# A factored interaction network on one core: the four 64-row matmuls of a pair, issued two and two instead of all together

## The chip, the core and the metric

The kernel runs on one core of a Trainium2 chip. The metric is the device time of one execution in microseconds (us). Three executions of the kernel before gave 449.19, 449.53 and 449.75 us, so the median is 449.53 us. The profile that the document reads is of one further execution, which took 450.12 us; the span that its trace covers is 448.3 us, and the 1.8 us between the two lie outside the records.

## What is computed

The reference is a "compressed interaction network" over x of shape (1024, 64, 16): three layers, each of which multiplies every field of x with every field of the layer's input and contracts the products with a weight matrix. Cut to what matters:

```python
x0 = h = x                                          # (B=1024, F=64, E=16)
for i in range(3):                                  # W0: 128 x 4096, W1 and W2: 128 x 4096
    z = einsum('bfe,bge->bfge', x0, h).reshape(B, F * fh, E)
    y = einsum('oc,bce->boe', W[i], z) + b[i]
    x_i, h = (y[:, :64], y[:, 64:]) if i < 2 else (y, y)
    xs.append(x_i)
out = concat(xs, 1).sum(axis=2) @ fc_w.T + fc_b     # (B, 1)
```

## The kernel before

All data is fp32. The batch is cut into 32 chunks of 32 rows; a chunk has 32 x 16 = 512 columns (batch and embedding together). The kernel doesn't form all products of fields: it lays x out so that a product of two 128-row tiles (`z` blocks of 128 x 4 x 512, made on VectorE and GpSimd) holds pairs of fields at a fixed distance, and TensorE contracts those blocks with rearranged weights (`w_all`, `ws`).

Six chunks are done by a head (chunks 0 to 5; the first of them also build the rearranged weights) and by a tail; the other 26 are done as 13 pairs, `k` = 3 to 15. A pair's two chunks share products and sums of products, so that some contractions serve both. Each contraction is a matmul of 128 rows (the partitions that are summed over) by 64 columns (outputs) over 512 moving columns. Two outputs of 64 columns lie in the two column halves of the array and of a PSUM bank: half 0 is output partitions 0 to 63, half 1 is 64 to 127. For a pair, `p["A"]` is the half of chunk `b`, `p["O"]` that of chunk `a`: `A` is half 0 for even `k` and half 1 for odd `k`. The sums lie in the PSUM banks `alpha` (L605), `delta` (L608), `gamma` (L611) and `beta` (L614), each in one half of its bank.

TensorE's order is written by hand. `at(when, fn, ...)` (L516) puts a job on a list with a time; at the end of `cin_kernel` the list is sorted by that time and each job is recorded in turn, so that `when` fixes the order of the instructions on every engine and nothing else. `zipped(when, columns...)` (L519) takes two lists of jobs and interleaves them: job `m` of the first list at `when + m`, job `m` of the second at `when + m + 0.5`. One such couple of jobs, one per column half, is called a slot here. `window` (L741) zips the two lists of one pair, `a_column` (everything that goes to half `A`) and `o_column` (everything that goes to half `O`), in such an order that the first list is always that of half 0. The 13 windows come from `first_window` (L748, `k` = 3), `o_leads` (L771, odd `k`) and `a_leads` (L759, even `k`), each with 29 slots, the first with 27.

Not every term has 128 rows. The squares of single fields (`es[c]`: x in partitions 0 to 63, x squared in 64 to 127) go through four matmuls of 64 rows by 64 columns for each pair, issued by `squares` (L734): `h_extra` (L565) multiplies the lower half of `es[c]` (rows 64 to 127) into `alpha` for chunk `b` and into `delta` for chunk `a`; `v0x` (L572) multiplies its upper half (rows 0 to 63) into a bank `y` of its own. Chunk `b`'s two write half `A`, chunk `a`'s two write half `O`. So the four cover the four quarters of the array, and `squares` issues them one after the other at `t + 22.9`, between slot 22 and slot 23 of the window (in the last window at `t + 30.2`, after its last slot).

Other engines work around this: VectorE makes the products (L642) and adds the factors (L680 to L690), ScalarE copies operands into PSUM (L554) and takes snapshots of the sums (L669 to L675), GpSimd adds and subtracts product blocks (`w_mix`, L651, its operation at L659), and SyncE issues the loads. A `z` block is handed out by `take` (L87) from the front of a list of free blocks, and comes back to its end by `used` (L92) when the last matmul that reads it has been recorded; so the order in which matmuls are recorded also settles which block a later product gets.

All matmuls of the windows go through `mm` (L525), so their rows in the profile have the line L526, and are told apart by their tiles: `alpha<-e,vs` and `delta<-e,vs` are the two of `h_extra`, `y<-e,v` the two of `v0x`.

Of the kernel before, what the change touches and what calls it, by code (L numbers as in the profile page):

```python
# [70 lines left out]
def cin_kernel(ctx, tc, xra, xrb, wh, w0r, w1h, w2t, wx1, wx0, vec, out):  # L71
# [297 lines left out]
    for h in range(2):  # L369
        at = slice(32 * h, 32 * h + 32)  # L370
# [145 lines left out]
    def at(when, fn, *args, **flags):  # L516
        ops.append((when, len(ops), fn, args, flags))

    def zipped(when, *columns):  # L519
        for n, column in enumerate(columns):  # L520
            for m, job in enumerate(column):
                if job is not None:
                    at(when + m + n / len(columns), *job)

    def mm(out, w, rhs, start=False, stop=False):  # L525
        nc.tensor.matmul(out, w, rhs, start=start, stop=stop, skip_group_check=True)  # L526
# [38 lines left out]
    def h_extra(c, out=None, start=False):  # L565
        out = accs[c] if out is None else out
        mm(out[halves[c % 2]], w0ds[halves[1]], es[c][halves[1]], start=start)

    def new_y(k, tag):
        ys[k] = ps.tile([128, N], F32, tag=tag, name=f"y_{k}", bufs=4 if tag == "acc" else 2)  # L570

    def v0x(c, tag):  # L572
        if c // 2 not in ys:
            new_y(c // 2, tag)
        mm(ys[c // 2][halves[c % 2]], v0[halves[0]], es[c][halves[0]], start=True, stop=True)
# [49 lines left out]
    def w_run(p, out, w, name, start=False, at_t=0, order=GROUPS):  # L625
        return [
            (w_job, p, out, w, j * NI + i + at_t, name, start and n == 0)
            for n, (j, i) in enumerate(order)
        ]

    def p1_run(p, order, start=True):
        return w_run(p, alpha, wq_all, "X", start, order=order)

    def p7_run(p, order, start=True):
        return w_run(p, delta, s3, "T3", start, order=order)
# [85 lines left out]
    def p4_run(p):  # L721
        return w_run(p, delta, wh_all, "T2", at_t=2 * NI)

    def first_fill(p):
        return [(lambda: q_extra(p["a"], va, p["beta"]),)] + p4_run(p)[-LATE : -LATE // 2]

    def second_fill(p):
        return p4_run(p)[-LATE // 2 :]

    def late_run(p, out=alpha, first=0, last=2 * NI):  # L730
        jobs = w_run(p, out, s4, "B22", out is gamma)[first:last]
        return jobs if last < 2 * NI else jobs + [(lambda: q_extra(p["b"], vb, p["alpha"]),)]

    def squares(p):  # L734
        a, b = p["a"], p["b"]
        h_extra(b, p["alpha"])
        h_extra(a, p["delta"])
        v0x(b, "set")
        v0x(a, "set")

    def window(t, p, a_column, o_column, p1, p7, u2, quads=22.9):  # L741
        zipped(t, *(a_column, o_column)[:: -1 if p["k"] % 2 else 1])
        at(t + quads, squares, p)
        at(t + p1 - 0.4, snap_p1, p)
        at(t + p7 - 0.2, snap_p7, p)
        at(t + u2 - 0.4, snap_u2, p)

    def first_window(t, p, after, left):  # L748
        window(
            t, p,  # L750
            p1_run(p, GROUPS) + left[1][:1] + [(q_extra, 4, va)] + w_run(p, alpha, s2, "T2")
            + left[1][1:] + w_run(p, alpha, s1, "T3"),
            p7_run(p, GROUPS) + left[0][:1] + [(q_extra, 5, va)]
            + w_run(p, beta, wq_all, "B21", True, 2 * NI) + left[0][1:]
            + p1_run(after, FIRST_ROW) + p4_run(p)[:-LATE],
            8, 8, 18,
        )

    def a_leads(t, p, before, after):  # L759
        fill = first_fill(before)  # L760
        window(
            t, p,
            p1_run(p, SECOND_ROW, False) + fill[:1] + w_run(p, alpha, s2, "T2", order=FIRST_ROW)
            + fill[1:] + w_run(p, alpha, s2, "T2", order=SECOND_ROW) + second_fill(before)
            + w_run(p, alpha, s1, "T3") + p7_run(after, FIRST_ROW),
            p7_run(p, GROUPS) + late_run(before) + w_run(p, beta, wq_all, "B21", True, 2 * NI)
            + p4_run(p)[:-LATE],
            4, 8, 15,
        )

    def o_leads(t, p, before, after):  # L771
        last = after is None
        window(
            t, p,
            p1_run(p, SECOND_ROW + FIRST_ROW) + first_fill(before) + w_run(p, alpha, s2, "T2")
            + second_fill(before) + w_run(p, alpha, s1, "T3"),
            p7_run(p, SECOND_ROW, False) + late_run(before)
            + w_run(p, beta, wq_all, "B21", True, 2 * NI)
            + (late_run(p, gamma, 0, NI) if last else p1_run(after, FIRST_ROW))
            + p4_run(p)[:-LATE],  # L780
            8, 4, 19, 30.2 if last else 22.9,
        )

    def end_pair(t, p, whens):
# [93 lines left out]
    for n, p in enumerate(pairs):  # L878
        t = T0 + SPAN * n
        q, after = pairs[n - 1], pairs[n + 1] if n + 1 < NPAIR else None  # L880
        if n == 0:
            load_pair(t, p, -39.9, -33.3, -39.8, -27)
            make_pair(
                t, p, (-23.4, -20.7, -20.4, -16.5, -17.2, -16.8, -16.6, -7, -13.5, 3),
                (-14, -6.9, -6.8, 7.2, 12.4, 17.6, 17.5),
            )
            first_window(
                t, p, after, [[(contract_half, 5, 3, i, h) for i in (2, 3)] for h in range(2)]
            )
        else:  # L890
            load_pair(t, p, -34, -28, -27.8, -27.7)
            make_pair(
                t, p, (-21.4, -18.7, -18.4, -15.8, -12.2, -9.5, -6.1, -2, 1.6, 4.2),
                (-5, 1.6, 3.6, 7.2, 12.4, 18.6, 18.5),
            )
            (a_leads if n % 2 else o_leads)(t, p, q, after)
            end_pair(t, q, (0.7, 11.7, 17.9, 22.3, 23.2, 18.4, 36))
# [40 lines left out]
    t, q = T0 + SPAN * NPAIR, pairs[-1]  # L938
# [98 lines left out]
    last = cuts[1]  # L1037
# [84 lines left out]
```

## Time and profile before

| what | value |
|---|---|
| executions | 449.19, 449.53, 449.75 us |
| median | 449.53 us |
| profiled execution, its own time | 450.12 us |
| its span | 448.3 us |
| TensorE (PE) busy | 443.8 us, 99% of the span |
| VectorE (DVE) busy | 391.3 us, 87% |
| GpSimd (POOL) busy | 364.4 us, 81% |
| ScalarE (ACT) busy | 115.8 us, 26% |
| granted TensorE clock | 1.00 |

The page gives for each engine the busy time, its share of the span and the number of instructions. "PE" is TensorE's matmuls, "PEld" its weight loads, which have records of their own. One fp32 matmul of the program is executed as two passes over its moving columns, and each pass has one record as a matmul and one as a weight load. The ends of matmuls are modelled (a pass over 512 columns is recorded as 0.59 us long, and the next one on the same half starts 0.43 us after it), so TensorE's pace is read from starts, not from durations. A row of the timeline gives the start in us from the start of the span, the duration, engine, line, operation, the tiles (written<-read), rows*columns of the array where it is TensorE, the shape and type, and how many equal records in sequence were merged.

### The profile page before, as it was taken

The page shows a single profiled execution, that of the slowest core. Times are in us where ns is not written, and L with a number is a line of the kernel's source. Part 1 is how long each engine was busy: PE and PEld are TensorE (multiplying, and loading weights), DVE is VectorE, ACT ScalarE, POOL GpSimd, SP SyncE. Part 2 cuts the span into 40 slices and gives each one's busy share as a digit, 9 for nine tenths or more (in the row PEclk, how much of TensorE's full clock was granted, in tenths as well). Part 3 has the DMA queues.
Part 4 walks back from the last instruction along what each step waited for, and adds up shares of the span by engine and source line. Part 5 has one row for each costly group of instructions (what it writes and reads, how often), then busy time and mean ns, then how long its engine had stood idle before and what let it go on. Part 6 is the DMA issues. An engine that isn't in the chain of part 4 may idle for free.

```text
span 448.3 us, 6065 instructions
## 1 busy us (share of the span) xinstructions
PE 443.8 (99%) x2302; PEld 166.3 (37%) x2302; DVE 391.3 (87%) x284; ACT 115.8 (26%) x215; POOL 364.4 (81%) x125
## 2 busy tenths in 40 slices
PE   8999999999999999999999999999999999999997
PEld 4466343333333334333333333333333333333345
DVE  3996499989989989999899979999899998999644
ACT  2153151332222223131222222222231312222211
POOL 5413699998997979899797989979798997979920
PEclk9999999999999999999999999999999999999999
DMA  8987899298939587694958869495876939682500
GB/s 296 415 299 172 312 415 361 80 347 146 351 97 298 182 209 270 135 362 97 283 193 203 289 122 361 105 289 181 210 272 137 371 89 277 240 223 94 107 0 2
DMA packets 34484, 99.67 MB, mean 222 GB/s; under 512 B 6324, under 2 KB 6996, under 8 KB 27864
## 3 DMA queue, kind: packets, MB, share of 16 engines
q1 hardware_dynamic: 31800, 84.70, 53.4%
q0 software_dynamic: 1872, 13.63, 17.2%
q10 hardware_dynamic: 784, 0.95, 0.8%
q8 instruction: 18, 0.29, 0.3%
q14 instruction: 10, 0.08, 0.1%
HBM read 84.00 MB, written 1.64 MB: 191 GB/s over the span
## 4 chain that ended last, share of the span: by engine, by line
PE 98%; POOL 1%; ACT 0%; DVE 0%; issue 0%; POOLq 0%
PE alpha L526 45%; PE delta L526 20%; PE beta L526 11%; PE acc L526 7%; PE acc L252 6%; PE q L526 3%; PE acc L270 3%; POOL z L242 1%; PE misc L115 1%; PE xp L221 1%; PE y L526 0%; PE pv L359 0%; PE pm L386 0%; PE hx L526 0%; ACT xb_gps L314 0%; PE pc L924 0%
## 5 line engine op out<-in xcount | busy, mean ns | idle before, releaser
L659 POOL TENSOR_TENSOR z<-z,z 128x2048 f32<-128x2048 f32 (+1 forms) x78 | 299.6, 3872 | 30.5 <-PE alpha L526 30.5
L526 PE MATMUL alpha<-z,ws 128*64 128x512 f32 x624 | 240.8, 593 | 0.0
L642 DVE TENSOR_TENSOR z<-xa,xp 128x2048 f32<-128x2048 f32 x103 | 231.5, 2279 | 1.2
L526 PEld LDWEIGHTS alpha<-z,ws 128*64 128x64 f32 x624 | 75.2, 137 | 87.5 <-issue 84.8
L526 PE MATMUL delta<-z,w_all 128*64 128x512 f32 x208 | 95.5, 592 | 0.0
L526 PE MATMUL alpha<-z,w_all 128*64 128x512 f32 x208 | 93.5, 594 | 0.0
L526 PE MATMUL beta<-z,w_all 128*64 128x512 f32 x208 | 92.7, 594 | 0.0
L526 PE MATMUL delta<-z,ws 128*64 128x512 f32 x208 | 92.1, 594 | 0.0
L554 ACT COPY xp<-xb 128x512 f32<-128x512 f32 x88 | 51.4, 586 | 129.3 <-DVE z L642 110.8
L242 DVE TENSOR_TENSOR z<-xa,xp 128x2048 f32<-128x2048 f32 (+2 forms) x23 | 45.0, 2002 | 6.1 <-ACT xp L554 4.6
L242 POOL TENSOR_TENSOR z<-xa,xb 128x2048 f32<-128x2048 f32 x6 | 27.5, 4645 | 19.4 <-DMA xb<-in_xrb 19.4
L526 PEld LDWEIGHTS alpha<-z,w_all 128*64 128x64 f32 x208 | 28.0, 137 | 32.3 <-issue 29.2
L526 PEld LDWEIGHTS delta<-z,w_all 128*64 128x64 f32 x208 | 28.4, 137 | 30.8 <-issue 30.8
L526 PEld LDWEIGHTS beta<-z,w_all 128*64 128x64 f32 x208 | 28.0, 137 | 27.4 <-issue 27.4
L526 PEld LDWEIGHTS delta<-z,ws 128*64 128x64 f32 x208 | 27.9, 137 | 27.4 <-issue 25.7
L252 PE MATMUL acc<-z,w_all 128*64 128x256 f32 x256 | 29.0, 381 | 1.3 <-DVE z L242 1.2
L526 PE MATMUL acc<-z,w_all 128*64 128x512 f32 (+1 forms) x96 | 28.4, 594 | 0.0
L252 PEld LDWEIGHTS acc<-z,w_all 128*64 128x64 f32 x256 | 18.0, 137 | 13.6 <-DVE z L242 2.7
L673 ACT ACTIVATE snap<-alpha,vs 64x512 f32<-64x512 f32 x13 | 8.9, 682 | 50.1 <-PE alpha L526 50.1
L680 DVE SCALAR_TENSOR_TENSOR snap<-alpha,vs,snap 64x512 f32<-64x512 f32 x13 | 9.7, 747 | 12.4 <-PE alpha L526 12.3
L670 ACT COPY snap<-alpha 64x512 f32<-64x512 f32 x13 | 7.5, 580 | 48.7 <-PE delta L526 34.4
L294 DVE TENSOR_REDUCE acc<-uu 128x64 f32<-128x1024 f32 (+2 forms) x19 | 19.6, 1036 | 0.2
(117 smaller groups left out, 355.8 us busy)
## 6 DMA issues: line engine op xcount, KB each, us to landing
xa<-in_xra SPq DMA_DIRECT2D x32, 1024.0 KB, 8.9
xb<-in_xrb SPq DMA_DIRECT2D x128, 256.0 KB, 8.2
z<-z POOLq DMA_DIRECT2D x13, 1024.0 KB, 8.4
e<-in_xra SPq DMA_DIRECT2D x28, 128.0 KB, 8.1
xx<-in_xra SPq DMA_DIRECT2D x28, 128.0 KB, 3.1
z<-in_w2t SPq DMA_DIRECT2D x2, 1024.0 KB
z<-in_wx SPq DMA_DIRECT2D x2, 1024.0 KB, 9.1
z<-in_w1h SPq DMA_DIRECT2D x1, 1024.0 KB
```

The costliest lines, as they stand in the source:

```text
L115: nc.tensor.matmul(misc[:, 0:n], zeros, zeros[:, 0:n], start=True, stop=True)
L242: engine.tensor_tensor(blocks[zs[c, j]][:, at, :], xas[c][:, at, :], xbs[c][j].unsqueeze(1).to_broadcast([128, last - first, N]), ALU.mult,)
L252: nc.tensor.matmul(accs[c][halves[n]], w_all[:, t, 0:64], blocks[zs[c, j]][:, i, n * H2 : (n + 1) * H2], start=(t == 0), stop=(j == last a ...
L270: nc.tensor.matmul(accs[c][halves[1 - c % 2]], w_all[:, t, 64:128], blocks[zs[c, j]][:, i, :], start=(t == 0), stop=False, skip_group_chec ...
L294: nc.vector.tensor_reduce(acc[rows, of, k, half], uu[rows, of if at is None else at, E * half.start : E * half.stop].rearrange("p k (b e) ...
L526: nc.tensor.matmul(out, w, rhs, start=start, stop=stop, skip_group_check=True)
L554: nc.scalar.copy(bank, xbs[c][j])
L642: engine.tensor_tensor(blocks[b], xas[c], xbs[c][j].unsqueeze(1).to_broadcast([128, NI, N]), ALU.mult)
L659: nc.gpsimd.tensor_tensor(*(blocks[b][:, first:last] for b in (o, x, y)), ALU.subtract if in1 == "T3" else ALU.add,)
L670: nc.scalar.copy(snaps[0][p["O"]], alpha(p))
L673: nc.scalar.activation(snaps[1][p["O"]], alpha(p), AF.Identity, bias=bh1[p["A"]])
L680: nc.vector.scalar_tensor_tensor(hb_, alpha(p), bh1[p["A"]], hb_, ALU.add, ALU.add)
```

## The change

`squares` now issues the two matmuls of one chunk only: `h_extra` and `v0x` of that chunk, which write the same column half. `window` splits the zipped lists at `cut`, which is slot 23: slots 0 to 22 are zipped as before. Then come the two 64-row matmuls of half 0's chunk (`order[0]`), the half-1 job of slot 23, the half-0 job of slot 23, the two 64-row matmuls of half 1's chunk (`order[1]`), and then the remaining slots, each with its half-1 job first. In the last window the lists end before the cut, so that there the four 64-row matmuls stay together, in a new order (half 0's two, then half 1's two). No instruction is added or taken away on any engine.

```diff
-    def squares(p):
-        a, b = p["a"], p["b"]
-        h_extra(b, p["alpha"])
-        h_extra(a, p["delta"])
-        v0x(b, "set")
-        v0x(a, "set")
-
-    def window(t, p, a_column, o_column, p1, p7, u2, quads=22.9):
-        zipped(t, *(a_column, o_column)[:: -1 if p["k"] % 2 else 1])
-        at(t + quads, squares, p)
+    def squares(p, c):
+        h_extra(c, p["alpha" if c == p["b"] else "delta"])
+        v0x(c, "set")
+
+    def window(t, p, a_column, o_column, p1, p7, u2, quads=22):
+        columns, order = (a_column, o_column), (p["b"], p["a"])
+        if p["k"] % 2:
+            columns, order = columns[::-1], order[::-1]
+        cut = min(quads + 1, len(columns[0]))
+        zipped(t, columns[0][:cut], columns[1][:cut])
+        at(t + quads + 0.9, squares, p, order[0])
+        for m in range(cut, len(columns[0])):
+            at(t + m - 0.04, *columns[1][m])
+            at(t + m + 0.04, *columns[0][m])
+            if m == cut:
+                at(t + m + 0.08, squares, p, order[1])
+        if cut == len(columns[0]):
+            at(t + quads + 0.95, squares, p, order[1])
         at(t + p1 - 0.4, snap_p1, p)
         at(t + p7 - 0.2, snap_p7, p)
         at(t + u2 - 0.4, snap_u2, p)
...
-            8, 4, 19, 30.2 if last else 22.9,
+            8, 4, 19, 29.3 if last else 22,
```

## The prediction, as it was put on record before the changed kernel ran

> **What bounds the kernel now.** I read three views, from the widest to the closest: the page's busy times and its chain of work, the busy times stage by stage, and the timeline of TensorE around one issue of `squares`.
>
> ```profile
> PE 443.8 (99%) x2302; PEld 166.3 (37%) x2302; DVE 391.3 (87%) x284; ACT 115.8 (26%) x215; POOL 364.4 (81%) x125
> ...
> PE 98%; POOL 1%; ACT 0%; DVE 0%; issue 0%; POOLq 0%
> ```
>
> The first line alone proves little, since matmul records are modelled long. The second does more: followed back from the last instruction, 98% of the span was spent on TensorE with nothing else to wait for. So what TensorE spends or saves in its own stream goes to the end, as long as the others keep up.
>
> ```profile
> 131.00:157.06 26.06, 26.06 (x126) 8.46 (x124) 24.99 (x19) 6.33 (x11) 23.49 (x8) 1.00 0.74 222
> 157.06:183.24 26.18, 26.18 (x126) 9.38 (x125) 23.65 (x17) 6.21 (x11) 23.77 (x8) 1.00 0.73 221
> ```
>
> These are two stages, each from one issue of the four 64-row matmuls to the next, with the busy times of PE, PEld, DVE, ACT and POOL after the length; then the granted clock (1.00, so nothing here is throttled). Each is 29 slots and one `squares`, and the stages from 131.0 to 392.2 us repeat these two lengths. VectorE and GpSimd have at least 1 us of air in 26; GpSimd waits for TensorE 12 times, 30.5 us together. They follow, TensorE leads.
>
> ```profile
> 130.01 0.59 PE L526 MATMUL alpha<-z,ws 128*64 128x512 f32 x1
> 130.05 0.59 PE L526 MATMUL beta<-z,w_all 128*64 128x512 f32 x1
> 130.44 0.59 PE L526 MATMUL alpha<-z,ws 128*64 128x512 f32 x1
> 130.48 0.59 PE L526 MATMUL beta<-z,w_all 128*64 128x512 f32 x1
> 131.00 0.64 PE L526 MATMUL alpha<-e,vs 64*64 64x512 f32 x1
> 131.01 0.64 PE L526 MATMUL delta<-e,vs 64*64 64x512 f32 x1
> 131.01 0.65 PE L526 MATMUL y<-e,v 64*64 64x512 f32 x2
> 131.48 0.59 PE L526 MATMUL alpha<-e,vs 64*64 64x512 f32 x1
> 131.49 0.59 PE L526 MATMUL delta<-e,vs 64*64 64x512 f32 x1
> 131.50 0.59 PE L526 MATMUL y<-e,v 64*64 64x512 f32 x2
> 132.02 0.64 PE L526 MATMUL alpha<-z,ws 128*64 128x512 f32 x1
> 132.03 0.64 PE L526 MATMUL beta<-z,w_all 128*64 128x512 f32 x1
> 132.50 0.59 PE L526 MATMUL alpha<-z,ws 128*64 128x512 f32 x1
> 132.51 0.59 PE L526 MATMUL beta<-z,w_all 128*64 128x512 f32 x1
> 132.93 0.59 PE L526 MATMUL alpha<-z,ws 128*64 128x512 f32 x1
> ```
>
> Read the starts. In the plain stream the two halves start together, and each half starts a pass every 0.43 us: between 116.28 and 125.72 us one half of this trace starts 22 passes later, 0.429 us each. A slot is two passes, 0.858 us. At the 64-row matmuls the four quarters start within 0.02 us, so the four cost one slot and not four. But the steps around them are longer: 130.48 to 131.00 is 0.52, to 131.48 is 0.48, to 132.02 is 0.54, to 132.50 is 0.48, and then 0.43 again. Against 0.429 that is 0.09 + 0.05 on the way in and 0.11 + 0.05 on the way out, 0.306 us together on the trace's finer starts: 0.153 us for each change between 128 rows and 64. The stage confirms it: 60 passes of 0.429 and 0.306 make 26.05 us, and 26.06 were seen.
>
> ```profile
> 130.05 0.14 PEld L526 LDWEIGHTS beta<-z,w_all 128*64 128x64 f32 x1
> 131.00 0.13 PEld L526 LDWEIGHTS alpha<-e,vs 64*64 64x64 f32 x1 [0.81 <-issue]
> ```
>
> The weight loads say what the time is. In the plain stream the weights of a pass are loaded while the pass before runs: the load at 130.05 is for the pass at 130.48. The load for the first 64-row pass stands at 131.00, when everything before it has gone through, although it waits for no other engine. And it belongs to half 0 (`k` = 4 is even, `alpha` is in half 0), whose last 128-row pass started at 130.44, 0.04 us before that of half 1. At the pass after a full 0.52 us (the distance seen from 130.48) half 0 could have begun at 130.96. It began at 131.00, in this pair and in the other even pairs alike (at 183.24 it is 182.68, 182.72 and 183.24). So the wait is for the whole array, not for the own half.
>
> **What the Trainium skill says.** "TensorEngine Tiling (Array Packing)", section Key Properties: "Changing tiling mode (not just tile) drains the TensorE"; its list of configurations has 128x64 and 64x64 as two modes. The trace agrees, with 0.153 us a change. "TensorE: Matmul & The Clock Gate", section Step-by-step, has weight loads pulled ahead of running matmuls while the matmuls keep the program's order. The trace agrees for the plain stream (130.05), and shows no load pulled ahead over a change of rows (131.00). Neither page says whether a 64-row tile may run beside a 128-row tile in other columns; that a mode belongs to the whole array is my reading of the drain and of the 0.04 us above.
>
> **The change, part by part.** It touches the 12 windows `k` = 3 to 14. In the 13th the four 64-row matmuls stay together; only their order differs, and they and the four of `end_squares` after them are all 64x64, with 0.02 us between the starts of four: nothing.
>
> *Removed:* per window one slot in which four 64-row matmuls run together, 0.858 us, and two changes of rows, 0.306.
>
> *Added:* half 0's two 64-row matmuls, one couple of 128-row matmuls, half 1's two. If the array has one mode at a time, the first two run alone with the other half empty: two passes, 0.858 us. Then a change, the couple, a change, the second two alone, 0.858 us again, a change. That is two slots and four changes (in, out, in, out) at 0.153: 1.716 + 0.612 = 2.328. The couple itself is an old slot and stays.
>
> *Difference:* 2.328 - (0.858 + 0.306) = 1.164 us a window, 12 windows: 13.97 us. Nothing hides it: it is TensorE's own stream.
>
> The price of a change beside another change isn't in the trace before. The lower bound is the first step alone without the 0.05 us on the second pass, about 0.1; the upper is 0.2, if both halves come staggered (at 106.31 us one half had started its last pass 0.73 us earlier instead of 0.52). I take 0.153, the value of each of the 12 places where it can be read. The ends: 0.858 + 4 x 0.1 - 0.306 = 0.95, or 0.858 + 4 x 0.2 - 0.306 = 1.35 a window, 11.4 and 16.2 us.
>
> *Moved:* the remaining slots have half 1's job ahead of half 0's; they start together anyway (0.01 us). Which `z` block comes free first changes, and with it the names that later products get; the order on VectorE, ScalarE, GpSimd and of the loads stays. I cost this at nothing: each new owner of a block still comes slots later, and a window that is 1.16 us longer gives GpSimd (2.4 us of wait a window already) and VectorE more air. If that cover failed, the price would be like the one wait of TensorE that the windows have, 26.18 against 26.06, 0.12 us in every other one, under 1 us in all. That wait itself stays: it is local to slots 1 to 5 of a window (GpSimd starts a half block at 165.25, takes 2.36, and TensorE goes on at 167.61), and no 64-row matmul lies between. The change adds no semaphore wait.
>
> Sum on the profiled execution: 450.12 + 13.97 = 464.1; it lies 0.59 above the median of the three runs, so against the median 449.53 + 13.97 = **463.5 us**. Both kernels' times outside the span I take as equal.
>
> **The rivals.**
>
> *Overlap without a price.* A mode is a matter of columns, and a half that changes rows is switched without the other noticing: half 0's two squares run beside half 1's job of slot 23, half 0's job of slot 23 beside half 1's two squares. Then the slots are as many as before (two half slots instead of one whole), and if the weights can also be loaded early the 0.306 us vanish: 12 x 0.306 = 3.67, 445.9 us, faster. It decides from the point where the array takes a 64-row and a 128-row tile at once. For it: the four quarters run together at 131.00, so tiles are independent to a degree. Against it: the load at 131.00, and the 0.04 us of the even pairs, which show half 0 waiting for half 1.
>
> *Overlap with a drain by halves.* Tiles of different rows run together, but each half drains when its own rows change, and since matmuls start in order the other half is held up too. There are three such points (in, the exchange, out) instead of two: 12 x 0.153 = 1.84, 451.4 us, slower by 0.4%. For it: as above, and the drain seen. Against it: the same 0.04 us.
>
> *A new wait.* The renamed blocks put GpSimd in TensorE's way: at most a few tenths a window on top of the forecast, inside the range.
>
> **How the numbers follow.** The whole array in one mode: 0.89, 463.5 us, with its own ends 449.53 + 11.4 = 460.9 and 449.53 + 16.2 = 465.7. Drain by halves: 0.04, 451.4. Overlap without a price: 0.05, 445.9. Something between the last two, within 0.2% of now: 0.02. The range 460.9 to 465.8 holds the first case nearly whole and leaves out the rest, about 0.13 in all. Slower by over 0.2% (0.9 us, about what a measurement of this kernel can tell from no change): 0.89 + 0.04 = 0.93; within: 0.02; faster: 0.05.
>
> **What would show it.** If I am right, the timeline after shows two `y` passes and two of one `e` chunk with no 128-row pass between or beside them for about 0.5 + 0.5 us, then two passes of one couple, then the other two; four long first steps of 0.52 to 0.54 us per window; stages of about 27.2 and 27.3 us. The wrong sign would show as 128-row records that start between the two passes of a 64-row matmul, 0.43 us apart, and stages of 25.75 us. Stages of 26.2 with three long steps would be the drain by halves. Stages beyond 27.6 would mean that a change costs more next to another one, or a wait by TensorE that the weight loads' idle times then name.

## The result, and the profile after

The changed kernel takes 463.48 us (median of 5 executions, 462.57 to 463.69) against 449.75 us for the kernel before (5 executions, 449.19 to 450.26). The medians differ by 13.7 us. The ratio on record is 1.0296, with a 95% interval from 1.0279 to 1.0312, which is 12.5 to 14.0 us: slower. (The two medians by themselves give 1.0305, inside it.) The forecast was 463.5 us. The profiled execution has a span of 461.6 us, 13.3 over before, and TensorE is busy for 457.1 us of it against 443.8, with the same 2302 matmul passes.

First the chain of work of the page, and the stages, each from one window's first 64-row matmuls to the next window's:

```profile
PE 97%; DMA 2%; SPq 0%; DVE 0%; issue 0%; ACT 0%; ACTq 0%
```

```profile
106.07:131.68 25.61, 25.61 (x119) 8.90 (x118) 22.62 (x18) 6.14 (x11) 21.95 (x6) 1.00 0.75 223
131.68:158.88 27.20, 27.20 (x127) 8.54 (x125) 25.07 (x19) 6.33 (x11) 23.47 (x8) 1.00 0.71 213
158.88:186.21 27.33, 27.33 (x127) 9.48 (x126) 23.66 (x17) 6.22 (x11) 23.77 (x8) 1.00 0.72 212
```

The chain is still TensorE's; the 2% of DMA are one load in the first 11 us, long before any changed instruction. The first stage shown starts at the first window and is shorter than the others before as after. The other two are longer by 27.20 - 26.06 = 1.14 us and by 27.33 - 26.18 = 1.15 us; VectorE (third of the busy times) and GpSimd (fifth) are as busy in them as before, to 0.1 us. So the added time is TensorE's own. Now the timeline of TensorE at the place that the prediction showed:

```profile
131.11 0.59 PE L526 MATMUL alpha<-z,ws 128*64 128x512 f32 x1
131.15 0.59 PE L526 MATMUL beta<-z,w_all 128*64 128x512 f32 x1
131.67 0.64 PE L526 MATMUL alpha<-e,vs 64*64 64x512 f32 x1
131.68 0.64 PE L526 MATMUL y<-e,v 64*64 64x512 f32 x1
132.15 0.59 PE L526 MATMUL alpha<-e,vs 64*64 64x512 f32 x1
132.16 0.59 PE L526 MATMUL y<-e,v 64*64 64x512 f32 x1
132.68 0.64 PE L526 MATMUL beta<-z,w_all 128*64 128x512 f32 x1
132.68 0.64 PE L526 MATMUL alpha<-z,ws 128*64 128x512 f32 x1
133.16 0.59 PE L526 MATMUL beta<-z,w_all 128*64 128x512 f32 x1
133.16 0.59 PE L526 MATMUL alpha<-z,ws 128*64 128x512 f32 x1
133.69 0.64 PE L526 MATMUL delta<-e,vs 64*64 64x512 f32 x1
133.69 0.64 PE L526 MATMUL y<-e,v 64*64 64x512 f32 x1
134.17 0.59 PE L526 MATMUL delta<-e,vs 64*64 64x512 f32 x1
134.17 0.59 PE L526 MATMUL y<-e,v 64*64 64x512 f32 x1
134.69 0.64 PE L526 MATMUL beta<-z,w_all 128*64 128x512 f32 x1
134.70 0.64 PE L526 MATMUL alpha<-z,ws 128*64 128x512 f32 x1
```

Between 131.67 and 132.68 only the two matmuls of one chunk run, in half 0; the `beta` job of half 1, next in the program, doesn't start beside them but at 132.68, together with half 0's own next job. The same again from 133.69 to 134.69 with the halves exchanged. The steps from one kind of rows to the other are 0.52 (131.15 to 131.67), 0.52, 0.53 and 0.52 us, four of them instead of two, and each is followed by one of 0.48; a plain step is 0.43. In none of the 13 windows of the changed kernel does a 128-row pass start within 0.4 us of the start of a 64-row pass.

### The profile page after: what moved, and what is told of

Same layout as the page of the kernel before. It is cut to its first block, busy times and chain, and to the rows that moved or that the text cites. A ratio compares the mean times of both kernels' runs of the same rounds, so it can differ in the third digit from the quotient of the medians.

```text
span 461.6 us, 6065 instructions
## 1 busy us (share of the span) xinstructions
PE 457.1 (99%) x2302; PEld 167.3 (36%) x2302; DVE 392.3 (85%) x284; ACT 115.8 (25%) x215; POOL 364.3 (79%) x125
## 4 chain that ended last, share of the span: by engine, by line
PE 97%; DMA 2%; SPq 0%; DVE 0%; issue 0%; ACT 0%; ACTq 0%
PE alpha L526 49%; PE delta L526 22%; PE acc L526 6%; PE acc L252 6%; PE beta L526 5%; PE q L526 3%; PE acc L270 3%; DMA z<-in_w0r 2%; PE y L526 0%; PE pm L386 0%; PE pv L359 0%; SPq L146 0%; PE xp L221 0%; PE hx L526 0%; PE pc L932 0%
## 5 line engine op out<-in xcount | busy, mean ns | idle before, releaser
L526 PE MATMUL alpha<-z,ws 128*64 128x512 f32 x624 | 243.3, 594 | 0.0
L526 PEld LDWEIGHTS alpha<-z,ws 128*64 128x64 f32 x624 | 74.2, 137 | 109.5 <-issue 108.3
L526 PE MATMUL alpha<-z,w_all 128*64 128x512 f32 x208 | 94.5, 594 | 0.0
L526 PE MATMUL beta<-z,w_all 128*64 128x512 f32 x208 | 93.9, 595 | 0.0
L526 PE MATMUL y<-e,v 64*64 64x512 f32 x64 | 29.5, 611 | 0.0
```

## The experiments

The theory: TensorE has one row mode at a time (128 rows or 64), for the whole array. A group of 64-row matmuls has the array to itself for its slot, whatever quarters of it are in use, and the array drains on the way in and on the way out: what runs has to finish before passes with other rows start. Then the change is one slot more and two changes of rows more in each of 12 windows. The rivals: the cost lies in the new order and the renamed blocks; in the one half that stands empty; or tiles of different rows do run together and each half drains by itself. The kernel before ran again beside the experiments: 449.65 us beside the slot alone, the split by rows and the runs of four, 449.78 us beside the other four. Below, "over before" is the difference from the median that goes with the run.

**The new order, with the four together.** From the changed kernel:

```diff
             at(t + m + 0.04, *columns[0][m])
-            if m == cut:
-                at(t + m + 0.08, squares, p, order[1])
-        if cut == len(columns[0]):
-            at(t + quads + 0.95, squares, p, order[1])
+        at(t + quads + 0.95, squares, p, order[1])
```

Expected:

> The changed kernel with its new order of jobs (half 0's two 64-row matmuls first, then half 1's; half 1's job first in the later slots; the renamed blocks), but with all four 64-row matmuls in a row. If the whole array has one mode at a time (theory), the four run together again: no slot and no change of rows more than before, so the time of before, 449.7 us. If the new order, or the blocks that it renames, carries a part of the cost (rival: a new wait), that part stays: clearly above 450.5 us.

Measured: 449.64 us, ratio 1.0002 (0.9987 to 1.0017). The order of the jobs, the half-1 job ahead in the later slots and the renamed blocks cost nothing that can be told from the noise; the 13.7 us hang on the couple of 128-row jobs between the two groups.

**All rows 128.** From the changed kernel, for the 12 windows; `hp` is a new tile with zeros in rows 0 to 63 and the weights of `h_extra` below, and the lower half of `v0` is set to zero:

```diff
-        h_extra(c, p["alpha" if c == p["b"] else "delta"])
-        v0x(c, "set")
+        bank = p["alpha" if c == p["b"] else "delta"]
...
+        mm(bank[halves[c % 2]], hp, es[c])
+        mm(ys[c // 2][halves[c % 2]], v0, es[c], start=True, stop=True)
```

Expected:

> The changed kernel's order, but in the 12 windows the four matmuls are widened to 128 rows, with weights whose other 64 rows are zero, so that no change of rows is left there. Theory (one mode for the whole array): half 0's two now run beside half 1's job, half 1's two beside half 0's; the four cost two slots in the plain stream, 1.716 us, against 1.164 before: 12 x 0.552 = 6.6 us over before, 456.4 us, and no long steps in the timeline. Rival (half of the array stays empty because of the order of the jobs or the banks that they write, not because of the rows): one half still idles, and the time stays near the changed kernel's 463.5 us less the drains, 12 x 0.6, thus about 456 only if the halves do overlap; if they don't, two lonely couples of slots (four slots, 3.43 us) give about 477 us.

Measured: 456.00 us, ratio 1.0131 (1.0112 to 1.0151), which is 6.2 us over before; the stages are 26.61 and 26.69 us, 0.55 and 0.51 over (two slots in place of one slot and two changes of rows, 1.716 - 1.164 = 0.552). At the group the halves now run side by side:

```profile
130.54 0.59 PE L531 MATMUL alpha<-e,hp 128*64 128x512 f32 x1
130.66 0.59 PE L531 MATMUL beta<-z,w_all 128*64 128x512 f32 x1
130.97 0.59 PE L531 MATMUL alpha<-e,hp 128*64 128x512 f32 x1
131.09 0.59 PE L531 MATMUL beta<-z,w_all 128*64 128x512 f32 x1
```

The same job of half 0, with the same input and the same output, has a half-1 job beside it (130.54 and 130.66) and no long step, as soon as it has 128 rows (L531 is `mm` in this kernel). The half-1 job starts at 130.66 ahead of half 0's second widened job (131.39), which stands before it in the program. So the rows are what keeps the halves apart in the changed kernel, not the order, the banks or the inputs. The change's arrangement with all rows 128 is 7.5 us faster than with 64, although half of its weights are zero, and still slower than the four quarters together.

**One slot more, no change of rows more.** The kernel before, in 12 windows:

```diff
-        v0x(b, "set")
-        v0x(a, "set")
+        for n in range(2 if p["k"] < 2 + NPAIR else 1):
+            v0x(b, "set")
+            v0x(a, "set")
```

Expected:

> One slot more, no change of rows more, without touching the order of the 128-row jobs: the kernel before, with the two matmuls of v0x issued twice in a row in 12 windows (the second overwrites the first with the same values). The group of 64-row matmuls then lasts two slots, with half of the array empty in the second. Theory: 0.858 us in 12 windows, 10.3 us, 460.1 us; with the 4.0 us of the run with two changes more, this gives 14.3, a little over the changed kernel's 13.7 because the one-column matmul has a time of its own. Rival (what is lost in the changed kernel is not the lonely 64-row slots but something beside them): clearly less than 10 us.

Measured: 459.69 us, ratio 1.0225 (1.0210 to 1.0240), 10.0 us over before. The stages:

```profile
130.96:157.88 26.92, 26.92 (x130) 8.73 (x128) 25.09 (x19) 6.33 (x11) 23.48 (x8) 1.00 0.72 215
157.88:184.92 27.04, 27.04 (x130) 9.63 (x129) 23.65 (x17) 6.22 (x11) 23.76 (x8) 1.00 0.73 214
```

Each is 0.86 over. This is the term of the slot. It is a price and doesn't decide between the theory and the rivals of overlap: the repeated `v0x` fill the upper quarters of both halves, so that no half stands free for a 128-row job.

**Two changes more, no slot more.** The kernel before, in 12 windows; `zeros` are the weights:

```diff
+    def change(p):
+        c = 2 * p["k"]
+        mm(ys[p["k"]][halves[0]][:, 0:1], zeros[halves[0], 0:F], es[c][halves[0], 0:1])
...
         at(t + quads, squares, p)
+        if p["k"] < 2 + NPAIR:
+            at(t + quads + 2, change, p)
```

Expected:

> Two changes of rows more than before, but no slot more: the kernel before, with one 64-row matmul over a single moving column (zero weights, added to a sum) two slots after the four, in 12 windows. Theory: two changes of 0.146 us (the value in the changed kernel's timeline) and next to nothing for the one column: 0.29 to 0.35 us in 12 windows, 3.5 to 4.2 us, 453.2 to 454.0 us, and both halves show the long step although only half 0 has the 64-row tile. Rival (a change costs only beside another one, or only where 512 columns follow): within 1 us of before. Together with the run with one slot more this should add up to the changed kernel's 13.7 us.

Measured: 453.82 us, ratio 1.0083 (1.0064 to 1.0101), 4.0 us over before; the stages are 26.41 and 26.53 us, both 0.35 over. In its timeline:

```profile
132.76 0.59 PE L526 MATMUL alpha<-z,ws 128*64 128x512 f32 x1
132.77 0.59 PE L526 MATMUL beta<-z,w_all 128*64 128x512 f32 x1
133.29 0.27 PE L526 MATMUL y<-e,const-float32-0.0 64*64 64x1 f32 x2
133.49 0.64 PE L526 MATMUL delta<-z,ws 128*64 128x512 f32 x1
133.50 0.64 PE L526 MATMUL delta<-z,w_all 128*64 128x512 f32 x1
133.97 0.59 PE L526 MATMUL delta<-z,ws 128*64 128x512 f32 x1
133.98 0.59 PE L526 MATMUL delta<-z,w_all 128*64 128x512 f32 x1
134.40 0.59 PE L526 MATMUL delta<-z,ws 128*64 128x512 f32 x1
```

One column of work, in one half, holds up both: the next passes of both halves start at 133.49 and 133.50, where the plain pace would have had them at 133.20. This is what one mode for the whole array gives. By itself it doesn't refute the drain by halves, which in the prediction's form has the other half held up too, by the order of the program; that rival falls by the timeline of the changed kernel, where no 128-row pass runs beside a 64-row one. Slot and changes add to 10.0 + 4.0 = 14.0 us, against the change's 13.7, and in a stage to 0.86 + 0.35 = 1.21 us, against 1.14 and 1.15. By estimate the one-column matmul has the rest as a time of its own: 0.35 less two changes of 0.146 us (the finer value of the changed kernel's timeline) is 0.06 us.

**Split by rows instead of by halves.** From the changed kernel: first both `h_extra`, then the couple of 128-row jobs, then both `v0x`:

```diff
-    def squares(p, c):
-        h_extra(c, p["alpha" if c == p["b"] else "delta"])
-        v0x(c, "set")
+    def squares(p, n):
+        for c in (p["b"], p["a"]):
+            if n == 0:
+                h_extra(c, p["alpha" if c == p["b"] else "delta"])
+            else:
+                v0x(c, "set")
...
-        at(t + quads + 0.9, squares, p, order[0])
+        at(t + quads + 0.9, squares, p, 0)
...
-                at(t + m + 0.08, squares, p, order[1])
+                at(t + m + 0.08, squares, p, 1)
...
```

Expected:

> The changed kernel, but the four 64-row matmuls are split the other way: first the two of h_extra (lower rows, both halves), then a couple of 128-row jobs, then the two of v0x (upper rows, both halves). Theory (a group of 64-row matmuls takes the whole array for its slot, whatever quarters it fills, and each group has two changes): the changed kernel's time, 463.5 us, within 0.5. Rival (the loss comes from one column half standing empty beside the 64-row matmuls of the other): here both halves are in use in each group, so less than 463.5 by several us.

Measured: 463.44 us, ratio 1.0310 (1.0294 to 1.0325): the changed kernel's time, with stages of 27.20 and 27.33 us like its own. Here each group uses both halves, and the cost is the same. So it doesn't come from one half standing empty. These two ways of splitting the four in two were tried, and no other.

**A 128-row job of half 1 ahead of the four, that of half 0 behind.** From the changed kernel; the later slots have half 0's job first again:

```diff
+        if cut < len(columns[0]):
+            at(t + quads + 0.85, *columns[1][cut])
         at(t + quads + 0.9, squares, p, order[0])
+        at(t + quads + 0.95, squares, p, order[1])
         for m in range(cut, len(columns[0])):
-            at(t + m - 0.04, *columns[1][m])
-            at(t + m + 0.04, *columns[0][m])
-            if m == cut:
-                at(t + m + 0.08, squares, p, order[1])
-        if cut == len(columns[0]):
-            at(t + quads + 0.95, squares, p, order[1])
+            at(t + m, *columns[0][m])
+            if m > cut:
+                at(t + m + 0.5, *columns[1][m])
```

Expected:

> One slot more than before, but no change of rows more: half 1's 128-row job of slot 23, then all four 64-row matmuls, then half 0's 128-row job of slot 23. Theory: the 128-row job runs alone, the four together, the other 128-row job alone; 0.858 us more than before in 12 windows, 10.3 us, 460.0 us. Rival (each half drains by itself, tiles of different rows overlap): half 1's job runs beside half 0's two and half 0's job beside half 1's two, with one change more: 12 x 0.15 = 1.8 us, 451.5 us. Rival (overlap without a price): about 446 us.

Measured: 456.48 us, ratio 1.0145 (1.0124 to 1.0165), 6.7 us over before: none of the three numbers. The timeline around the group:

```profile
130.48 0.59 PE L526 MATMUL alpha<-z,ws 128*64 128x512 f32 x1
130.51 1.45 PE L526 MATMUL beta<-z,w_all 128*64 128x512 f32 x3
131.90 0.64 PE L526 MATMUL alpha<-e,vs 64*64 64x512 f32 x1
131.90 0.64 PE L526 MATMUL y<-e,v 64*64 64x512 f32 x1
131.91 0.64 PE L526 MATMUL delta<-e,vs 64*64 64x512 f32 x1
...
132.91 0.64 PE L526 MATMUL alpha<-z,ws 128*64 128x512 f32 x1
132.93 0.64 PE L526 MATMUL beta<-z,w_all 128*64 128x512 f32 x1
133.39 0.59 PE L526 MATMUL alpha<-z,ws 128*64 128x512 f32 x1
```

Half 0 is done at the pass of 130.48; half 1 (`beta`) goes on for two passes more, alone; only then do the 64-row matmuls start, those of half 0 included: at 131.90, where 0.52 us after half 0's own last pass would have been 131.00. So the group waits for the other half here too. What the expectation missed is that the lone job of half 0 behind the group isn't alone. At 132.93 the next `beta` job starts beside its first pass, ahead of the `alpha` job (in the program between the two) that half 0 only comes to later. Half 1 thereby stays a job ahead, and the stages alternate:

```profile
131.90:158.16 26.26, 26.26 (x125) 10.14 (x125) 24.41 (x18) 6.33 (x11) 22.83 (x7) 1.00 0.73 220
158.16:185.20 27.04, 27.04 (x126) 10.05 (x125) 24.32 (x18) 6.21 (x11) 24.34 (x10) 1.00 0.69 214
```

In the first, the next group finds half 1 ahead by most of a slot, so its extra job there is covered, and 0.20 us is lost. In the second, a wait at 168.7 us brings both halves level (the next two jobs of both start at 168.74), and the next group pays the whole slot, 27.04 - 26.18 = 0.86. From the first group to the last, 106.58 to 429.60 us, this comes to 323.02 - 317.10 = 5.9 us (317.10 is the same stretch before); what the first group itself costs lies ahead of that stretch.

**Runs of four jobs per half.** Whether jobs really start ahead of their turn, and how far, was tried on the kernel before, in slots 8 to 15 of 11 windows:

```diff
-        zipped(t, *(a_column, o_column)[:: -1 if p["k"] % 2 else 1])
+        columns = (a_column, o_column)[:: -1 if p["k"] % 2 else 1]
+        if p["k"] in (3, 2 + NPAIR):
+            zipped(t, *columns)
+        else:
+            for n, column in enumerate(columns):
+                for m, job in enumerate(column):
+                    run = 8 <= m < 16
+                    at(t + (m - m % 4 + n * 2 + m % 4 / 4 if run else m + n / 2), *job)
```

Expected:

> Asks why the run with one half's job ahead of the four cost 6.7 us and not 10.3: its timeline shows a half-1 job starting ahead of a half-0 job that stands before it in the program. The kernel before, with slots 8 to 15 of 11 windows issued as four jobs of half 0, four of half 1, four of half 0, four of half 1. If matmuls start strictly in program order, eight slots take thirteen: 5 x 0.858 x 11 = 47 us more, about 497 us. If each half has a queue of its own that holds at least three waiting jobs, nothing is lost: 449.7 to 450.5 us. In between if the queue is shorter.

Measured: 470.45 us, ratio 1.0474 (1.0455 to 1.0492), 20.8 us over before, which is 1.9 us or 2.2 slots in each of 11 windows: in between. The first runs of one window in the timeline:

```profile
199.82 0.59 PE L526 MATMUL alpha<-z,ws 128*64 128x512 f32 x1
199.83 0.59 PE L526 MATMUL alpha<-z,w_all 128*64 128x512 f32 x1
200.25 2.31 PE L526 MATMUL alpha<-z,ws 128*64 128x512 f32 x5
201.97 0.64 PE L526 MATMUL beta<-e,va 128*64 128x512 f32 x1
202.39 0.59 PE L526 MATMUL alpha<-z,ws 128*64 128x512 f32 x1
...
203.25 0.59 PE L526 MATMUL alpha<-z,ws 128*64 128x512 f32 x1
203.31 1.02 PE L526 MATMUL delta<-z,w_all 128*64 128x512 f32 x2
203.74 0.64 PE L526 MATMUL alpha<-e,vb 128*64 128x512 f32 x1
```

Half 0's run has eight passes from 200.25 on. Half 1's first job (`beta<-e,va`) starts beside the fifth of them, when three of the run have not begun. Half 0's next run (`alpha<-e,vb`) starts at 203.74 beside the fifth pass of half 1's, and half 1's next at 205.56, again beside a fifth. So in this window a job started when three earlier passes of the other half still waited, and at none of the three places with more. The four passes that half 1 stands idle ahead of 201.97, 4 x 0.429 = 1.72 us, are most of the 1.9 us.

## Why the prediction was right

*What bounds the kernel.* Right: the stages grew by TensorE's own time and nothing else did. GpSimd's wait for TensorE went from 30.5 to 44.0 us in 12 waits, 1.1 us more each: the others had the air that the prediction gave them.

*One mode for the whole array.* Right, and no longer only read from 0.04 us: in the timeline after, half 1 starts nothing between 131.15 and 132.68; the matmuls widened to 128 rows overlap at once; one column in half 0 stops both halves; and with half 1's job ahead of the four, half 0 waits 0.90 us for it. What is shown is that in the windows of these kernels passes of 128 and of 64 rows never run together. Whether the array itself or the issue of its instructions keeps them apart, the traces don't tell.

*The slot, 0.858 us.* Measured alone as 0.86 a stage.

*The change of rows, 0.153 us.* A little less: in the changed kernel 0.52 + 0.48 - 2 x 0.429 = 0.142 on the two printed starts, 0.146 on the finer ones. The value from before was taken at groups of four, whose last starts 0.020 us after the first; in a group of two it is 0.006 us, and the step out, 0.52 us, counts from the last. A window costs 0.858 + 4 x 0.146 - 0.306 = 1.14 us, as the stages show, not 1.164. Twelve windows of it are 13.7 us.

*Twelve windows, 13.97 us.* A little too much, by the change of rows and by one term left out. The hit of 463.48 on 463.5 us is luck to that degree: against the 449.75 us of the five executions 13.73 us were added, and the forecast added its 13.97 to the lower 449.53. In the two profiled executions the span grew by 13.3 us. From the first group to the last the time is 436.69 - 106.07 = 330.62 us, against 423.41 - 106.31 = 317.10 before, so 13.52 us: 11 stages of 1.145 on average and a first one of 0.92. In the first window before, TensorE waits at 110.99 us (0.61 us from the pass before, and then 0.48, so 0.23 us lost); after, this wait isn't there, and that was not in the forecast. (The run with the slot alone loses it too: its first stage is 0.63 us over, the later ones 0.86.) The remaining 0.24 us (106.31 - 106.07) lie ahead of any changed instruction.

*What was costed at nothing.* The new order and the renamed blocks, rightly: 449.64 against 449.78 us with the four together. The wait in every other window stayed, 27.33 - 27.20 = 0.13 us.

*The rivals.* Drain by halves and free overlap both need a 128-row pass beside a 64-row one; there is none in the timeline after. The prediction had one thing wrong in how it described the first of them: "since matmuls start in order the other half is held up too". Three experiments (the widened rows, one job ahead, runs of four) show one half starting up to three passes ahead of its turn in the program. The forecast didn't rest on it, and in the changed kernel it didn't help, since both halves start level after each change of rows.

No run beat the kernel before. Its four quarters in one slot with two changes, 0.858 + 0.306 = 1.164 us a window, are the cheapest form that was tried: widened to 128 rows the four take two slots (1.716 us), and a split takes two slots and four changes (2.30 us).

## What to carry to other kernels

In this kernel (fp32, 512 columns a pass) matmuls of 64 rows didn't fill the empty half of the array beside matmuls of 128 rows: a group of 64-row tiles took the whole array for 0.86 us, with two quarters in use as with four, and each change of rows cost about 0.15 us. So gather the small ones until they fill all quarters at once, and count the groups, not the matmuls. Before splitting such a group to balance two halves, look at the step from the last common pass to the first small one. Here it told the outcome: the small matmul waited for the other half too, and its weights were loaded only then.

## What the runs showed that was not expected

Two column halves with equal rows aren't tied to each other's place in the program pass by pass. In the run with one half's job ahead of the four, a half-1 job started at 132.93 us beside the pass of 132.91, ahead of a half-0 job that stands earlier in the program; in the runs of four, half 1 started when three earlier passes of half 0 were still to come (201.97 us), after it had stood idle for four; and with all rows 128, a half-1 job started at 130.66 us, ahead of half 0's second widened job. "TensorE: Matmul & The Clock Gate" of the Trainium skill, section Step-by-step, says that matmuls stay in program order and only weight loads are pulled ahead; the three timelines here show starts out of that order between halves, and for them the measurement decides. So a job without a partner costs nothing while its half may run ahead; in the run with one job ahead it cost its slot where a wait had brought the halves level before the next group (0.86 us against 0.20).
